# Selective scans in a decoder: one state per step on 128 channels, or four states of 32 channels

## The chip, the cores and the metric

The kernel runs on one NeuronCore of a Trainium2 chip. The core has five engines that run side by side, each from its own queue in order: TensorE (PE in the profile, with its weight loads PEld as a row of their own), VectorE (DVE), ScalarE (ACT), GpSimd (POOL) and SyncE (SP), which issues the DMA transfers. The metric is the device time of one execution in microseconds. Before the change it is 2396.54 us, the median of three runs (2393.58 to 2400.45).

## The reference

Ten layers of a decoder on `x` of 4 sequences x 256 tokens x 256 channels, each ending in a layer norm of the sum. The change touches two of them, `L0_xattn` and `L1_xattn`, both selective state-space layers over the context. Cut to what matters:

```python
u = silu(conv4(in_proj_w @ ctx) + conv_b)               # 256 channels, 256 times, per sequence
dt_lo, Bm, Cm = split(x_proj_w @ u, (8, 16, 16))        # 16 states
delta = softplus(dt_proj_w @ dt_lo + dt_proj_b)
A = -exp(A_log)                                         # 256 channels x 16 states
for t in range(256):
    state = state * exp(delta[t] * A) + (delta[t] * u[t]) * Bm[t]
    y[t] = sum over the 16 states of state * Cm[t]
out = (y + D * u) * silu(x)
```

So for each of 4 sequences, 256 channels and 16 states there is a recurrence over 256 times, and the 16 states of a channel are summed at the end. The layers between them are a multi-query attention (before the first one), a small recurrent block called "thought" and a grouped attention (before the second one), and a mixture of experts after it.

## The kernel before

`Scans` (line 406) holds what the two state-space layers share. `load` brings the weights of a layer, `taps` (431) multiplies the four taps of the convolution with the input projection, so that `conv4(in_proj_w @ ctx)` becomes four matrix products. `_steps` (460) is a Python generator which emits a layer's instructions piece by piece, so that other code can put them beside its own. First it makes `u`, `delta` and `du` = `delta * u`, all with 128 channels on the partitions, two chunks of channels (`DC` = 2) and all 1024 times (4 sequences x 256) along the columns; B and C go to DRAM (`bc`).

Then comes one step for each sequence and state, 64 in a layer. A step loads the B and the C row of its state from DRAM, spread over all 128 partitions (tile `t` named `bc`, 256 KB, four buffers); ScalarE makes `exp(delta * A)` of both chunks (`dA`, three buffers); VectorE multiplies `du` by B into `s`, runs the scan over 512 columns (two chunks of 256 times; a zero in the first column of `dA` starts each chunk afresh), and multiplies by C. Two steps later (`late`) PE adds `s` into a PSUM bank by a product with the identity (`add`, 510). The bank sums the 16 states. After the last state VectorE adds `D * u` and leaves the result in `u`. There is one PSUM bank for all of this (`bank`, 441).

Who calls it: the first layer is begun inside the multi-query attention (`run_mqa`, 367) and goes on with `K.scans.beside(2)` (387) in each of its 32 iterations, two steps an iteration. The second is begun in `run_thought` (727), gets 24 steps at the end of that function (802), and one step at a time in the grouped attention (`run_gqa`, 1059 and 1063). `gate_pair` (549) multiplies a sequence's result by `silu(x)` and adds it to the stream; it first draws on the generator until that sequence is done (`upto`).

The order in which instructions are emitted is a priority and not yet the order on the engines: the framework plans each engine's queue at build time, with its own model of durations, and may move an instruction of a lower priority into a gap that it expects. On the chip each engine then runs its queue strictly in order. This holds for SP as well: a transfer whose memory or data is not ready yet holds up all that are issued after it. Helpers: `K.act` is a ScalarE activation (line 131), `K.tt`, `K.stt`, `K.ts` VectorE operations (116, 125, 120), `K.ptt` GpSimd (128), `K.mm` a matrix product (137). An fp32 matrix product shows as two MATMUL instructions and two weight loads. `again(ap, n)` reads the same columns n times.

Of the kernel before, what the change touches and what calls it, by code (L numbers as in the profile page):

```python
# [19 lines left out]
F32 = mybir.dt.float32  # L20
# [382 lines left out]
SSM_COLS = 19  # L403


class Scans:
    def __init__(self, K, ctx):
# [3 lines left out]
        self.wk = ctx.enter_context(tc.tile_pool(name="ssm2", bufs=4))  # L411
# [3 lines left out]
        self.dA = [self.one.tile([P, DC, L], F32, name=f"dA{k}") for k in range(3)]  # L415
# [6 lines left out]
    def load(self, pre):  # L422
        K = self.K
        self.w[pre] = {
            "in": K.load(self.one, f"{pre}_in", [P, D]),
            "xp": K.load(self.one, f"{pre}_xp", [P, DC, 40], "(c p) n -> p c n", p=P),
            "dt": K.load(self.one, f"{pre}_dt", [8, D]),
            "cols": K.load(self.one, f"{pre}_cols", [P, DC, SSM_COLS], "(c p) n -> p c n", p=P),
        }

    def taps(self, pre):
        K = self.K
        w = self.w[pre]
        w["taps"] = []
        for j in range(4):
            t = self.wk.tile([P, D], F32, name="tap", tag="bc", padded_shape=[P, 2 * L])
            K.nc.sync.dma_start(out=t, in_=K.A[f"{pre}_cw"][:, j * D : (j + 1) * D].to_broadcast([P, D]))
            K.ptt(t, t, w["in"], MUL)
            w["taps"].append(t)
# [20 lines left out]
    def _steps(self, pre):  # L460
        K, nc, w, wk = self.K, self.K.nc, self.w[pre], self.wk
# [3 lines left out]
        delta = self.one.tile([P, DC, N], F32, name="delta")  # L465
        du = self.one.tile([P, DC, N], F32, name="du")
# [5 lines left out]
        for h in range(2):  # L472
            for c in range(DC):
                ps = self.bank()
                for j in range(4):
                    K.mm(ps, taps[j][:, c * P : (c + 1) * P], K.ctxp[:, 2 * h : 2 * h + 2, j : j + L], j == 0, j == 3)
                K.act(u[:, c, 512 * h : 512 * h + 512], ps, AF.Identity, bias=cols[:, c, 0:1])
        K.act(u, u, AF.Silu)
        negA = self.one.tile([P, DC, 16], F32, name="negA")
        K.act(negA, cols[:, :, 2:18], AF.Exp)  # L480
        K.ts(negA, negA, -1.0, None, MUL)
        bc = self.dram.tile([2, 16, N], F32, name="bcd")
        for h in range(2):
            s = slice(512 * h, 512 * h + 512)
            xd = wk.tile([P, 512], F32, name="xd", tag="s")
# [6 lines left out]
            for c in range(DC):  # L492
# [3 lines left out]
                K.ts(delta[:, c, s], ps, cols[:, c, 1:2], None, ADD)  # L496
                K.act(du[:, c, s], ps, AF.Abs, bias=cols[:, c, 1:2])
        K.act(du, du, AF.Exp, scale=-1.0)
        K.act(du, du, AF.Ln, bias=K.eps[1.0])
        for c in range(DC):  # L500
            K.stt(delta[:, c, :], delta[:, c, :], 0.0, du[:, c, :], MAX, ADD)
            K.tt(du[:, c, :], delta[:, c, :], u[:, c, :], MUL)

        turn = 0
        self.y = u

        late = []
        bank = {}

        def add(b, n, s):  # L510
            if n == 0:
                bank[b] = self.bank()
            y = bank[b]
            K.mm(y, K.ident, s.rearrange("p c l -> p (c l)"), n == 0, n == 15)
            if n == 15:
                for c in range(DC):
                    v = u[:, c, b * L : (b + 1) * L]
                    K.stt(v, v, cols[:, c, 18:19], y[:, c * L : (c + 1) * L], MUL, ADD)
                self.done += 1

        for b in range(B):
            lo = b * L
            for n in range(16):
                yield
                if len(late) > 1:
                    add(*late.pop(0))
                t = wk.tile([P, 2, L], F32, name="bc", tag="bc")
                nc.sync.dma_start(out=t, in_=bc[:, n, lo : lo + L].unsqueeze(0).to_broadcast([P, 2, L]))
                dA = self.dA[turn % 3]
                turn += 1  # L530
                for c in range(DC):
                    K.act(dA[:, c, 1:L], delta[:, c, lo + 1 : lo + L], AF.Exp, scale=negA[:, c, n : n + 1])
                s = wk.tile([P, DC, L], F32, name="s")
                K.tt(s, du[:, :, lo : lo + L], again(t[:, 0, :], DC), MUL)
                nc.vector.tensor_tensor_scan(  # L535
                    out=s.rearrange("p c l -> p (c l)"),
                    data0=dA.rearrange("p c l -> p (c l)"),
# [1933 lines left out]
```

## Time and profile before

| what | value |
|---|---|
| median of three runs | 2396.54 us |
| the profiled execution | 2403.96 us, span 2402.2 us |
| granted TensorE clock, mean | 0.947 |
| 0 to 64 us | loads, first products of attention, `u`, `delta`, `du` of the first layer |
| 64 to 347 us | scans of the first layer, beside the multi-query attention |
| 347 to 409 us | end of attention, `u`, `delta`, `du` of the second layer, start of "thought" |
| 409 to 441 us | scans of the second layer beside "thought" |
| 441 to 468 us | end of "thought" |
| 468 to 701 us | scans of the second layer, beside the grouped attention from about 495 |

How to read it. "Busy" is the time in which an engine runs an instruction; a group row gives the line, the engine, the operation, the tiles written and read, the shapes (partitions x columns), the count, the busy time in us and the mean duration in ns, then the idle time of the engine before these instructions and what ended it. A row of the timeline begins with start and duration in us. A row of the waits says who waited for whom, the sum in us, how often, and the longest. In a row on stretches of time, "(x...)" is the number of instructions, and the numbers after the engines are the granted clock of TensorE, the DMA share and GB/s.

### The profile page before, as it was taken

The page shows a single profiled execution, that of the slowest core. Times are in us where ns is not written, and L with a number is a line of the kernel's source. Part 1 is how long each engine was busy: PE and PEld are TensorE (multiplying, and loading weights), DVE is VectorE, ACT ScalarE, POOL GpSimd, SP SyncE. Part 2 cuts the span into 40 slices and gives each one's busy share as a digit, 9 for nine tenths or more (in the row PEclk, how much of TensorE's full clock was granted, in tenths as well). Part 3 has the DMA queues.
Part 4 walks back from the last instruction along what each step waited for, and adds up shares of the span by engine and source line. Part 5 has one row for each costly group of instructions (what it writes and reads, how often), then busy time and mean ns, then how long its engine had stood idle before and what let it go on. Part 6 is the DMA issues. An engine that isn't in the chain of part 4 may idle for free. (4 is left out here: it accounts for less than half of the span.)

```text
span 2402.2 us, 28595 instructions
## 1 busy us (share of the span) xinstructions
PE 2227.1 (93%) x10504; PEld 1516.5 (63%) x10504; DVE 1461.9 (61%) x3178; ACT 787.2 (33%) x1763; POOL 260.4 (11%) x419
## 2 busy tenths in 40 slices
PE   8899998589987999899999999999999988899998
PEld 4566763335434655536888888888776545477676
DVE  4999975999876121380465544445565658686466
ACT  5677765223432011261211111111122223253443
POOL 1000010220010322200101000110110001200001
PEclk9999998788987999999999999999998888999999
DMA  7222221222213644220222111111100021100000
GB/s 224 62 55 60 48 66 31 56 70 53 49 36 94 195 129 125 77 72 5 75 86 87 47 47 56 66 47 49 48 22 1 1 77 43 42 1 1 1 1 18
DMA packets 133747, 139.50 MB, mean 58 GB/s; under 512 B 13892, under 2 KB 121766, under 8 KB 131944
## 3 DMA queue, kind: packets, MB, share of 16 engines
q1 hardware_dynamic: 133608, 137.68, 20.0%
q8 instruction: 83, 1.36, 0.2%
q14 instruction: 56, 0.46, 0.1%
HBM read 134.79 MB, written 2.85 MB: 57 GB/s over the span
## 5 line engine op out<-in xcount | busy, mean ns | idle before, releaser
L137 PE MATMUL ps<-xw,xcT 128*128 128x256 f32 (+1 forms) x2304 | 518.9, 382 | 0.3 <-ACT YT L131 0.3
L137 PEld LDWEIGHTS ps<-xw,xcT 128*128 128x128 f32 x2304 | 430.8, 190 | 64.0 <-issue 1.9
L116 DVE TENSOR_TENSOR xp<-ps,xb 128x256 f32<-128x256 f32 x96 | 40.5, 422 | 232.1 <-PE ps L137 232.0
L137 PE MATMUL sc<-kT,qT 32*128 32x256 f32 (+2 forms) x768 | 167.5, 412 | 10.0 <-DVE qn L134 9.7
L131 ACT ACTIVATE dA<-delta,negA 128x255 f32<-128x255 f32 x256 | 118.5, 501 | 131.1 <-DVE s L535 129.4
L137 PE MATMUL ssmps<-s,idz 128*128 128x512 f32 x256 | 143.7, 670 | 17.1 <-DVE s L116 16.0
L535 DVE TENSOR_TENSOR_SCAN s<-dA,s 128x512 f32<-128x512 f32 x128 | 154.6, 1219 | 2.6
L137 PEld LDWEIGHTS sc<-kT,qT 32*128 32x128 f32 (+1 forms) x768 | 106.9, 204 | 73.4 <-issue 45.2
L116 DVE TENSOR_TENSOR hT<-u,a 128x512 f32<-128x512 f32 x48 | 33.2, 691 | 186.0 <-PE u L137 184.9
L131 ACT ACTIVATE sq<-xp 128x1024 f32<-128x1024 f32 x24 | 25.4, 1057 | 314.1 <-DVE xp L116 314.1
L174 POOL TENSOR_SCALAR rstd<-mv 128x2 f32<-128x2 f32 x48 | 11.6, 241 | 951.9 <-DVE mv L166 932.7
L134 DVE TENSOR_REDUCE qn<-sc 128x2 f32<-128x480 f32 (+1 forms) x192 | 87.2, 506 | 39.1 <-PE sc L137 38.1
L131 ACT ACTIVATE e<-sT 128x512 f32<-128x512 f32 x128 | 70.9, 590 | 112.0 <-PE sT L137 109.9
L137 PE MATMUL sT<-q,kT 32*128 32x256 f32 (+1 forms) x384 | 103.4, 518 | 3.4 <-ACT e L131 3.3
L1503 DVE TENSOR_TENSOR_SCAN dec<-xT,idz 128x256 f32<-128x256 f32 (+1 forms) x192 | 89.8, 537 | 19.0 <-DMA xT<-ad 19.0
L131 ACT ACTIVATE a<-g 128x512 f32<-128x512 f32 x48 | 28.7, 599 | 206.4 <-PE g L137 206.4
L137 PE MATMUL g<-xT,wj 128*128 128x512 f32 x192 | 92.1, 603 | 0.7 <-ACT rows L105 0.7
L137 PE MATMUL u<-xT,wj 128*128 128x512 f32 x192 | 90.9, 595 | 0.0
L137 PEld LDWEIGHTS y<-wj,hT 128*128 128x128 f32 x384 | 73.0, 190 | 26.6 <-issue 18.2
L116 DVE TENSOR_TENSOR s<-du,bc 128x512 f32<-128x512 f32 x128 | 87.7, 694 | 2.7 <-PE ssmps L137 2.5
L137 PE MATMUL ps<-xT,wi 128*128 128x512 f32 x192 | 85.7, 603 | 4.0 <-ACT xin L131 4.0
L137 PE MATMUL y<-wj,hT 128*128 128x256 f32 x384 | 89.2, 379 | 0.0
(504 smaller groups left out, 4057.4 us busy)
## 6 DMA issues: line engine op xcount, KB each, us to landing
bc<-bcd SPq DMA_DIRECT2D x128, 256.0 KB, 4.5
xw<-in_l2a_xw_dram SPq DMA_DIRECT2D x24, 768.0 KB, 4.9
xT<-ad SPq DMA_DIRECT2D x12, 1024.0 KB, 4.5
wj<-in_l1f_gate_dram SPq DMA_DIRECT2D x48, 128.0 KB, 2.9
wj<-in_l1f_up_dram SPq DMA_DIRECT2D x48, 128.0 KB, 2.8
wj<-in_l1f_down_dram SPq DMA_DIRECT2D x48, 128.0 KB, 3.0
sel<-cwd SPq DMA_DIRECT2D x32, 192.0 KB, 3.3
sel<-cwd SPq DMA_DIRECT2D x32, 128.0 KB, 3.2
```

What stands on the lines that cost most here:

```text
L116: self.nc.vector.tensor_tensor(out=out, in0=a, in1=b, op=op)
L131: self.nc.scalar.activation(out, in_, func, **kw)
L134: self.nc.vector.tensor_reduce(out=out, in_=in_, axis=AX.X, op=op, **kw)
L137: self.nc.tensor.matmul(out, lhsT=lhsT, rhs=rhs, start=start, stop=stop)
L174: self.nc.gpsimd.tensor_scalar(out=out, in0=in_, scalar1=add, scalar2=None, op0=ADD)
L535: nc.vector.tensor_tensor_scan(out=s.rearrange("p c l -> p (c l)"), data0=dA.rearrange("p c l -> p (c l)"), data1=s.rearrange("p c l -> p ...
L1503: nc.vector.tensor_tensor_scan(out=dec[:, k, h, :], data0=ap[:, h, at(bb, k, j) : at(bb, k, 2)], data1=K.idz[:, 0 : (2 - j) * P], initial=0.0,
```

## The change

A step now holds 32 channels x 4 states on the 128 partitions (partition 4 x channel + state) and four groups of 32 channels along the columns, each with its 256 times: 1024 columns. A step is one sequence, one chunk of 128 channels and one set of four states: 4 x 2 x 4 = 32 steps in a layer. The number of scanned values is the same.

For that `delta` and `du` must be spread over four partitions per channel. They are put side by side in the tile `pair` (one per chunk), stored to DRAM (`dd`, 1 MB a chunk), and loaded back for each sequence and chunk with every channel's row repeated four times: eight loads of 128 KB into the new `t` (two buffers, shared with `pair` and `taps`), which serves the four steps of its chunk. B and C of four states are loaded once per sequence (`bct`, one buffer for each set, two loads of 128 KB), spread over 32 channels, and serve both chunks. `dA` has two buffers of 1024 columns, `s` four. The generator now yields twice in a step: before the loads, exponentials and product with B, and again before `add`, the scan and the product with C; so a call of `beside(1)` emits half a step, and there are still 64 calls in a layer.

The sum over the states is now also a sum over four partitions. `pick` is a matrix of zeros with a 32-column band in the middle that takes partition 4 c + state to column c. In the first layer each group's product has only the 32 columns of the band and writes 32 partitions of the bank; in the second layer each group takes 128 columns of `pick`, shifted so that the band lies at the group's 32 partitions and the rest adds zeros. Both are four products of 256 columns a step. The Exp and Ln of softplus run for each chunk apart.

```diff
-SSM_COLS = 19
+SSM_COLS = 3
+SN = 4
...
-        self.wk = ctx.enter_context(tc.tile_pool(name="ssm2", bufs=4))
+        self.wk = ctx.enter_context(tc.tile_pool(name="ssm2", bufs=2))
+        self.sp = ctx.enter_context(tc.tile_pool(name="ssm3", bufs=4))
...
-        self.dA = [self.one.tile([P, DC, L], F32, name=f"dA{k}") for k in range(3)]
+        self.dA = [self.one.tile([P, 4, L], F32, name=f"dA{k}") for k in range(2)]
...
+            "alog": K.load(self.one, f"{pre}_alog", [P, DC * 16]),
         }
+        if not hasattr(self, "pick"):
+            self.pick = K.load(self.one, "ssm_pick", [P, 2 * P - 32])
...
-        w["taps"] = []
+        w["taps"] = self.wk.tile([P, 4, D], F32, name="taps", tag="dd", padded_shape=[P, 8, D])
         for j in range(4):
-            t = self.wk.tile([P, D], F32, name="tap", tag="bc", padded_shape=[P, 2 * L])
+            t = w["taps"][:, j, :]
...
         bc = self.dram.tile([2, 16, N], F32, name="bcd")
+        dd = self.dram.tile([D, 2, N], F32, name="ddd")
+        pair = [self.wk.tile([P, 2, N], F32, name="pair", tag="dd") for _ in range(DC)]
...
-                K.ts(delta[:, c, s], ps, cols[:, c, 1:2], None, ADD)
-                K.act(du[:, c, s], ps, AF.Abs, bias=cols[:, c, 1:2])
-        K.act(du, du, AF.Exp, scale=-1.0)
-        K.act(du, du, AF.Ln, bias=K.eps[1.0])
+                K.ts(pair[c][:, 0, s], ps, cols[:, c, 1:2], None, ADD)
+                K.act(pair[c][:, 1, s], ps, AF.Abs, bias=cols[:, c, 1:2])
         for c in range(DC):
-            K.stt(delta[:, c, :], delta[:, c, :], 0.0, du[:, c, :], MAX, ADD)
-            K.tt(du[:, c, :], delta[:, c, :], u[:, c, :], MUL)
+            K.act(pair[c][:, 1, :], pair[c][:, 1, :], AF.Exp, scale=-1.0)
+        for c in range(DC):
+            K.act(pair[c][:, 1, :], pair[c][:, 1, :], AF.Ln, bias=K.eps[1.0])
+        for c in range(DC):
+            delta, du = pair[c][:, 0, :], pair[c][:, 1, :]
+            K.stt(delta, delta, 0.0, du, MAX, ADD)
+            K.tt(du, delta, u[:, c, :], MUL)
+            nc.sync.dma_start(out=dd[c * P : (c + 1) * P], in_=pair[c])
...
-        def add(b, n, s):
-            if n == 0:
+        def add(b, c, m, s):
+            if (c, m) == (0, 0):
                 bank[b] = self.bank()
             y = bank[b]
-            K.mm(y, K.ident, s.rearrange("p c l -> p (c l)"), n == 0, n == 15)
-            if n == 15:
+            for g in range(4):
+                at = slice(c * L, (c + 1) * L)
+                if pre == "l0x":
+                    K.mm(y[32 * g : 32 * g + 32, at], self.pick[:, P - 32 : P], s[:, g, :], c + m == 0, c + m == 4)
+                else:
+                    lo = P - 32 - 32 * g
+                    K.mm(y[:, at], self.pick[:, lo : lo + P], s[:, g, :], c + m + g == 0, (c, m, g) == (1, 3, 3))
+            if (c, m) == (DC - 1, 3):
...
         for b in range(B):
-            lo = b * L
-            for n in range(16):
-                yield
-                if len(late) > 1:
-                    add(*late.pop(0))
-                t = wk.tile([P, 2, L], F32, name="bc", tag="bc")
-                nc.sync.dma_start(out=t, in_=bc[:, n, lo : lo + L].unsqueeze(0).to_broadcast([P, 2, L]))
-                dA = self.dA[turn % 3]
-                turn += 1
-                for c in range(DC):
-                    K.act(dA[:, c, 1:L], delta[:, c, lo + 1 : lo + L], AF.Exp, scale=negA[:, c, n : n + 1])
-                s = wk.tile([P, DC, L], F32, name="s")
-                K.tt(s, du[:, :, lo : lo + L], again(t[:, 0, :], DC), MUL)
-                nc.vector.tensor_tensor_scan(
...
-                K.tt(s, s, again(t[:, 1, :], DC), MUL)
-                late.append((b, n, s))
+            at = slice(b * L, (b + 1) * L)
+            for c in range(DC):
+                for m in range(4):
+                    yield
+                    if m == 0:
+                        t = self.wk.tile([P, 2, 4, L], F32, name="dd", tag="dd")
+                        for j in range(2):
+                            for g in range(4):
+                                rows = dd[c * P + 32 * g : c * P + 32 * g + 32, j, at]
+                                nc.sync.dma_start(out=t[:, j, g, :], in_=rows.unsqueeze(1).to_broadcast([32, SN, L]))
+                    if c == 0:
+                        bct = self.one.tile([P, 2, L], F32, name=f"bct{m}")
+                        for k in range(2):
+                            rows = bc[k, SN * m : SN * m + SN, at]
+                            nc.sync.dma_start(out=bct[:, k, :], in_=rows.unsqueeze(0).to_broadcast([32, SN, L]))
+                        sets = [bct] if m == 0 else sets + [bct]
+                    dA = self.dA[turn % 2]
+                    turn += 1
+                    for g in range(4):
+                        q = 16 * c + 4 * g + m
+                        K.act(dA[:, g, 1:L], t[:, 0, g, 1:L], AF.Exp, scale=negA[:, q : q + 1])
+                    s = self.sp.tile([P, 4, L], F32, name="s")
+                    K.tt(s, t[:, 1], again(sets[m][:, 0, :], 4), MUL)
+                    yield
+                    if len(late) > 1:
+                        add(*late.pop(0))
+                    flat = s.rearrange("p g t -> p (g t)")
+                    nc.vector.tensor_tensor_scan(
...
+                    K.tt(s, s, again(sets[m][:, 1, :], 4), MUL)
+                    late.append((b, c, m, s))
```

## The prediction

> **What bounds the kernel now.** I read the page first, then busy time by stretches, the same for the scan tile `s` alone, the groups with shapes kept apart, the timeline of a dense stretch, and last the DMA issues and SP's waits. The page's shares and VectorE's busy tenths (one digit per 60 us):
> ```profile
> PE 2227.1 (93%) x10504; PEld 1516.5 (63%) x10504; DVE 1461.9 (61%) x3178; ACT 787.2 (33%) x1763; POOL 260.4 (11%) x419
> DVE  4999975999876121380465544445565658686466
> ```
> The 93% of PE is an average over the whole program. The change touches the first 720 us only, and there VectorE's digits are the nines. By stretches (us; PE, weight loads, DVE, ACT, POOL busy; clock; DMA), first for everything, then for tile `s` (PE, weight loads, DVE):
> ```profile
> 64.00:346.00 282.00, 264.64 (x1168) 184.61 (x1169) 267.80 (x445) 200.38 (x574) 11.51 (x18) 0.99 0.25 58
> 409.00:441.00 32.00, 24.44 (x119) 10.88 (x120) 28.85 (x45) 19.69 (x40) 2.77 (x2) 0.79 0.38 85
> 441.00:468.00 27.00, 7.44 (x30) 5.01 (x28) 24.42 (x74) 2.40 (x5) 14.09 (x22) 0.66 0.06 9
> 500.00:700.00 200.00, 187.64 (x1027) 89.99 (x1026) 178.66 (x288) 79.72 (x162) 21.16 (x42) 0.86 0.23 49
> ```
> ```profile
> 64.00:346.00 282.00, 60.57 (x128) 23.44 (x128) 156.80 (x192) 0.99 0.25 58
> 409.00:441.00 32.00, 14.41 (x22) 4.25 (x22) 28.02 (x36) 0.79 0.38 85
> 441.00:468.00 27.00, 0.00 (x0) 0.00 (x0) 1.60 (x2) 0.66 0.06 9
> 500.00:700.00 200.00, 47.84 (x74) 12.67 (x74) 102.00 (x118) 0.86 0.23 49
> ```
> The first layer's scans lie in 64 to 346 beside the first attention, the second layer's in 409 to 701. VectorE is busy 267.8 of 282 us in the first, and more than half of that is scans. PE is nearly as full, but VectorE has only 14.2 us of gaps. From 409 to 441 VectorE does almost nothing but scans; from 441 to 468 it has none.
>
> What one step costs. Groups (count, busy us, mean ns), then a dense stretch of the timeline (start, us), where steps follow each other with no wait:
> ```profile
> L535 DVE TENSOR_TENSOR_SCAN s<-dA,s 128x512 f32<-128x512 f32 x128 | 154.6, 1219 | 2.6
> L1503 DVE TENSOR_TENSOR_SCAN dec<-xT,idz 128x256 f32<-128x256 f32 x96 | 60.3, 674 | 19.0 <-DMA xT<-ad 19.0
> L116 DVE TENSOR_TENSOR s<-du,bc 128x512 f32<-128x512 f32 x128 | 87.7, 694 | 2.7 <-PE ssmps L137 2.5
> L116 DVE TENSOR_TENSOR prod<-rows,hot 128x1024 f32<-128x1024 f32 x4 | 4.9, 1220 | 2.9 <-ACT rows L105 2.8
> ```
> ```profile
> 414.61 0.67 DVE L116 TENSOR_TENSOR s<-du,bc 128x512 f32<-128x512 f32 x1
> 415.19 0.69 DVE L116 TENSOR_TENSOR s<-s,bc 128x512 f32<-128x512 f32 x1
> 415.79 1.22 DVE L535 TENSOR_TENSOR_SCAN s<-dA,s 128x512 f32<-128x512 f32 x1
> 416.93 0.67 DVE L116 TENSOR_TENSOR s<-du,bc 128x512 f32<-128x512 f32 x1
> ```
> From start to start a step takes 416.93 - 414.61 = 2.32 us, though its three durations add to 2.58: each instruction overlaps the next by 0.087 us. So VectorE pays little per instruction, and much per column.
>
> **The change, part by part.**
>
> (1) VectorE: two steps of 512 columns become one of 1024. A 1024-column product is 1.22 us (row `prod`). No scan of 1024 is in the trace; from 256 to 512 columns a scan grows by 545 ns, so 512 more add 1.09: 2.31 us. The big step is 1.22 + 1.22 + 2.31 = 4.75, less three overlaps of 0.087 = 4.49, against 2 x 2.32 = 4.64. That saves 0.15 x 32 steps = 4.8 us a layer, 9.6 in both. By durations without overlap (694 + 1219 + the 686 of the other product = 2.60 a step) it would be 5.20 - 4.75 = 0.45, 14.3 a layer: the upper bound. The lower bound is a loss: where a scan follows its own product, as at 338.98 to 339.70, nothing overlaps, and big steps of 4.75 in such a row would cost 0.11 more than two small ones overlapped, 3.5 a layer. I take 4.8, since the stretches that count run dense.
> [...]
>
> (2) The start of each layer. Before, the first product (64.1 in the first layer) follows 0.5 us after `du` is complete. Now `delta` and `du` go through DRAM. The Ln is split by chunk; a 1024-column ACT instruction takes 1.06 (row `sq`) where the 2048-column one took 2.00, so chunk 0 of the pair is ready at about 60.4 in place of 63.6. Then: the issue 0.4, the 1 MB store, then eight loads of `t` and two of `bct` on SP, 0.45 each = 4.5, and the last lands 2.9 later. SP also issues the second 1 MB store ahead of these loads. For the store I have transfers of 1 MB:
> ```profile
> xT<-ad SPq DMA_DIRECT2D x12, 1024.0 KB, 4.5
> wj<-in_l1f_gate_dram SPq DMA_DIRECT2D x48, 128.0 KB, 2.9
> w_d<-in_l0f_d_dram SPq DMA_DIRECT2D x1, 1024.0 KB, 8.1
> ```
> First product at 60.8 + 4.5 + 7.4 = 72.7, or 76.3 with 8.1: 8.6 to 12.2 us late; I take 10.4 (the second store is between). At worst the 14.9 us of the loaded `x` transfer: 19. In the first layer attention's VectorE work fills some of it: scans are 156.8 of 282 there, so 56% is lost, +5.8 (bounds 0, if attention runs ahead, and 19). In the second, scans are 28.0 of 32 us and nothing replaces them: +9.1 (0 to 19).
>
> (3) SP's order. In the second layer SP stood still, and the scan loads behind it:
> ```profile
> SPq L148 <- DVE gate L125: 25.2, 1, 25.2
> ```
> This is the router's load waiting for memory; the hole at 441 to 468 is its trace. One `t` now covers four big steps and there are two; `bct` covers two chunks. Steps can go on through the hole, and VectorE's idle there is 27 - 24.4 = 2.6: -2.6 (0 to -2.6). In the steady run, a layer issues 64 + 32 loads where it issued 64, 96 x 0.45 = 43 us of SP time in some 280: no bound. Single-buffered `bct` m is freed three steps before its next use (13 us or more, against 3 to 4.5 to land), `t` four steps before: no wait. The two loads more ahead of the taps push these back by 0.9: +0.5 (0 to 0.9).
>
> (4) PE. First layer: the four 512-column instructions of two steps take 1.88 us; eight band instructions, by this row of another stage,
> ```profile
> 590.22 1.05 PE L137 MATMUL o<-e,vt 128*32 128x256 f32 x16
> ```
> about 0.6, since four bands run at once. PE gets 32 x 1.28 = 41 us free, off the path: VectorE's waits for PE between 64 and 346 add to 1.5 us. -1.5 (0 to -14.2, all of VectorE's gaps). Second layer: eight of 256 columns at full width take 1.89 as in attention's rows, as much as four of 512: 0.
> PE's granted clock is 0.99 where PE is 94% busy and 0.66 where it is 28% busy. The bands take 41 us of its 264.6 away. At the clock of 500 to 700 the rest would need 224 x 0.99/0.86 = 258 us, still under VectorE's; at 0.79 it would need 281 and be level.
> [...]
>
> (5) Larger blocks in VectorE's queue. A reduction behind a scan waits up to 2.31 in place of 1.22. Between 500 and 700 lie 118/6 = 20 big steps: 0 to 20 x 1.09 = 22 us, and no gain, since no bank comes free earlier. VectorE works meanwhile; loss comes only when PE, freed late, leaves it dry. PE's weight loads waited 9.7 us for `qn` there, 14 times: I take +2. ACT's exponentials are as many and as long; two `dA` of a big step hold more than three small ones: 0.
>
> Sum: -9.6 + 5.8 + 9.1 - 2.6 + 0.5 - 1.5 + 2 = +3.7. The profiled execution took 2403.96 (span 2402.2 and 1.8 around it), 7.4 above the median of 2396.5: 2407.7 by it, 2400 by the median. 0.3% (7 us) is about what a measurement tells from no change.
>
> **The rivals.**
> Faster: the round trips are hidden. For: attention's work can run ahead of scans that are late, and the second layer has 2.6 + 21 us of idle later. Against: at 409 nothing else is ready. Without terms (2), -9.6 - 2.6 - 1.5 + 2 = -12: 2385; with the 14.3 of the durations in both layers, 2366.
> Slower: the blocks decide. One mechanism: in the second attention the score reductions stand behind 2.3 us scans, PE cannot refill its three score banks, VectorE runs dry when the scan is over. For: PE is busy 187.6 and VectorE 178.7 of 200, so neither has room, and the clock is already 0.86. Against: scans can be moved between reductions. 20 blocks at 1.09 less the 2 counted: +20, 2420. It decides from 11 us, half of that, on.
> The change moves nothing: VectorE's sum falls only by instruction overheads, and the starts give this back: 2390 to 2404, inside my forecast.
>
> **How the numbers follow.** Forecast, a draw with a small loss, 2389 to 2410: 0.47, of which 0.25 within 0.3% and 0.22 slower. Faster rival, 2366 to 2389: 0.33. Slower rival, 2410 to 2425 and above: 0.20. So faster 0.33, same 0.25, slower 0.42. The range leaves out a tenth on each side: 2378 to 2424; the likeliest case alone has 2389 to 2410.
>
> **What would show it.** Scans of 1024 columns at 2.3 us and products at 1.22; first product of a layer 8 to 12 us after `du`; between 64 and 346 PE's busy time some 40 us lower at a clock still near 0.99, the stretch about 280 long; scans going on while the router's load waits; PE's waits for `qn` near 10 us. I am wrong if VectorE stands idle behind `t` loads in the middle of a layer, if the clock in the first layer falls under 0.8, or if scans take other than 2.1 ns a column.

## The result, and the profile after

The changed kernel takes 2417.98 us in the median of 18 runs (2402.98 to 2436.44), the kernel before 2403.39 us beside it (18 runs, 2393.36 to 2413.92). The ratio is 1.0067, with a 95% interval of 1.0039 to 1.0095: slower by some 16 us. The profiled execution took 2433.68 us (span 2431.9). Executions of one kernel spread over 16 to 36 us here, and in the profiles up to 20 us of this lie behind the two layers, in code that no kernel here changes: from the first weight load of a later stage (`xw`) to the end it is 1292 to 1295 us in most, 1312 in three, this one among them, and 1301 in that of before. So I compare lengths of stages up to that mark as well as medians.

Three stages hold the change: A, up to SP's load of the grouped attention's weights (end of the first attention); B, from there to the load of the router's weights (thought); C, from there to the load of `sim` (the grouped attention). Their ends before are 353.27, 464.76 and 713.10 us, after 348.72, 456.25 and 731.85. Busy time by stage (us; PE, weight loads, VectorE, ScalarE, GpSimd; clock, DMA share, GB/s), A counted from 64 us. Before:

```profile
64.00:353.27 289.27, 271.91 (x1199) 189.77 (x1200) 268.67 (x447) 202.04 (x577) 12.78 (x19) 0.99 0.25 57
353.27:464.76 111.49, 77.01 (x360) 38.66 (x359) 72.89 (x162) 47.24 (x75) 22.37 (x35) 0.84 0.20 46
464.76:713.10 248.34, 224.96 (x1160) 105.45 (x1161) 216.14 (x353) 93.35 (x191) 27.19 (x52) 0.85 0.24 53
```

After:

```profile
64.00:348.72 284.72, 258.45 (x1346) 172.86 (x1345) 265.06 (x355) 202.55 (x594) 22.46 (x19) 0.97 0.18 47
348.72:456.25 107.53, 74.67 (x348) 39.94 (x346) 55.69 (x132) 43.55 (x66) 22.09 (x35) 0.79 0.20 60
456.25:731.85 275.60, 244.16 (x1302) 146.82 (x1303) 224.67 (x287) 97.70 (x203) 26.71 (x52) 0.80 0.13 35
```

A is 4.6 us shorter, B 4.0 shorter, C 27.3 longer: +18.7. Now take VectorE's busy time from each length. Its work shrank by 557.7 - 545.4 = 12.3 us. Its idle time went from 20.6 to 19.7 in A, from 38.6 to 51.8 in B, and from 32.2 to 50.9 in C: +31.0. So VectorE has less to do, as the larger instructions should give, and more idle time came in, none of it in the first layer's stage A. In stage C the last product of the layer ends at 701.00 us before, at 706.61 after: of the 27.3 us, 14.1 lie ahead of that product and 13.1 behind it, where VectorE has little left to do.

The lines that answer those of the prediction are these. The stretches for everything, then for tile `s` (PE, weight loads, VectorE):

```profile
64.00:346.00 282.00, 255.85 (x1329) 170.89 (x1327) 264.12 (x353) 202.55 (x594) 22.46 (x19) 0.97 0.18 47
409.00:441.00 32.00, 22.14 (x122) 13.05 (x122) 19.06 (x36) 16.34 (x32) 7.00 (x10) 0.71 0.32 99
441.00:468.00 27.00, 10.69 (x35) 7.33 (x36) 23.51 (x60) 1.23 (x3) 10.06 (x16) 0.56 0.05 10
500.00:700.00 200.00, 187.19 (x1049) 110.67 (x1049) 171.23 (x228) 76.41 (x162) 20.77 (x42) 0.81 0.12 32
```

```profile
64.00:346.00 282.00, 24.04 (x248) 5.86 (x248) 152.00 (x96) 0.97 0.18 47
409.00:441.00 32.00, 2.16 (x8) 1.44 (x8) 11.46 (x7) 0.71 0.32 99
441.00:468.00 27.00, 5.67 (x16) 3.83 (x16) 6.98 (x6) 0.56 0.05 10
500.00:700.00 200.00, 43.86 (x141) 30.82 (x141) 95.50 (x62) 0.81 0.12 32
```

Between 409 and 441 VectorE has 11.5 us of scan work where it had 28.0. Three big steps, as wide as six small ones, are scanned before the router's load, where 13 small ones were.

The groups (count, busy us, mean ns), and a dense stretch of VectorE's timeline (start, us):

```profile
L560 DVE TENSOR_TENSOR_SCAN s<-dA,s 128x1024 f32<-128x1024 f32 x64 | 146.3, 2292 | 6.0 <-ACT dA L131 5.0
L116 DVE TENSOR_TENSOR s<-dd,bct 128x1024 f32<-128x1024 f32 x64 | 77.9, 1226 | 12.5 <-PE ssmps L137 12.0
```

```profile
463.35 2.35 DVE L116 TENSOR_TENSOR s<-dd,bct 128x1024 f32<-128x1024 f32 x2
465.62 4.47 DVE L560 TENSOR_TENSOR_SCAN s<-dA,s 128x1024 f32<-128x1024 f32 x2
470.00 2.34 DVE L116 TENSOR_TENSOR s<-s,bct 128x1024 f32<-128x1024 f32 x2
472.25 2.35 DVE L116 TENSOR_TENSOR s<-dd,bct 128x1024 f32<-128x1024 f32 x2
```

Two big steps take 472.25 - 463.35 = 8.90 us, 4.45 each. The second row of the groups shows a wait of VectorE's: the first product of a step needs a free `s`, and PE's sum is what frees it.

SP's queue and VectorE's at the start of the second layer, and last VectorE's first product there before:

```profile
403.68 5.43 SPq L510 DMA_DIRECT2D ddd<-pair  x2
409.20 11.26 SPq L542 DMA_DIRECT2D dd<-ddd  x16
```

```profile
419.67 3.50 DVE L116 TENSOR_TENSOR s<-dd,bct 128x1024 f32<-128x1024 f32 x3
424.96 2.29 DVE L560 TENSOR_TENSOR_SCAN s<-dA,s 128x1024 f32<-128x1024 f32 x1 [1.80 <-ACT dA L131]
```

```profile
409.41 0.69 DVE L116 TENSOR_TENSOR s<-du,bc 128x512 f32<-128x512 f32 x1
```

Both stores and the second chunk's eight loads are in front, and a load of `dd` takes SP 11.26 / 16 = 0.70 us. The first product starts at 419.67, where it started at 409.41.

VectorE's waits for PE's sums in stage C (who for whom, us, times, longest), before:

```profile
DVE u L125 <- PE ssmps L137: 8.0, 2, 6.9
DVE s L116 <- PE ssmps L137: 2.3, 3, 1.6
```

and after:

```profile
DVE u L125 <- PE ssmps L137: 14.1, 3, 11.8
DVE s L116 <- PE ssmps L137: 12.0, 8, 2.6
```

One is the wait for a finished bank, the other that for a free buffer `s`. Together they are 26.1 us against 10.3.

### The profile page after: what moved, and what is told of

Its sections match the earlier page's. It is cut to its first block, busy times and chain, and to the rows that moved or that the text cites. A ratio compares the mean times of both kernels' runs of the same rounds, so it can differ in the third digit from the quotient of the medians.

```text
span 2431.9 us, 28936 instructions
## 1 busy us (share of the span) xinstructions
PE 2241.8 (92%) x10760; PEld 1546.1 (64%) x10760; DVE 1447.4 (60%) x2986; ACT 786.3 (32%) x1770; POOL 269.5 (11%) x418
## 5 line engine op out<-in xcount | busy, mean ns | idle before, releaser
L137 PE MATMUL sc<-kT,qT 32*128 32x256 f32 (+2 forms) x768 | 182.0, 437 | 14.9 <-DVE qn L134 9.8
L137 PEld LDWEIGHTS sc<-kT,qT 32*128 32x128 f32 (+1 forms) x768 | 113.1, 215 | 77.9 <-issue 44.8
L560 DVE TENSOR_TENSOR_SCAN s<-dA,s 128x1024 f32<-128x1024 f32 x64 | 146.3, 2292 | 6.0 <-ACT dA L131 5.0
L131 ACT ACTIVATE dA<-dd,negA 128x255 f32<-128x255 f32 x256 | 112.6, 500 | 97.6 <-DVE s L560 97.5
L137 PE MATMUL ssmps<-s,w_ssm_pick 128*32 128x256 f32 (+1 forms) x512 | 103.8, 431 | 22.2 <-DVE s L116 21.1
L174 POOL TENSOR_SCALAR rstd<-mv 128x2 f32<-128x2 f32 x48 | 12.1, 252 | 955.3 <-DVE mv L166 925.1
L137 PEld LDWEIGHTS ssmps<-s,w_ssm_pick 128*32 128x32 f32 (+1 forms) x512 | 62.7, 171 | 56.7 <-DVE s L116 29.3
```

Of the source, the lines that this page charges most:

```text
L131: self.nc.scalar.activation(out, in_, func, **kw)
L137: self.nc.tensor.matmul(out, lhsT=lhsT, rhs=rhs, start=start, stop=stop)
L174: self.nc.gpsimd.tensor_scalar(out=out, in0=in_, scalar1=add, scalar2=None, op0=ADD)
L560: nc.vector.tensor_tensor_scan(out=flat, data0=dA.rearrange("p g l -> p (g l)"), data1=flat, initial=0.0, op0=MUL, op1=ADD,)
```

## Experiments

First all of them. Each median stands beside that of the kernel before in the same session (2398.65 for the first four, 2403.67 for the next four, 2404.20 for e9 to e11, 2404.42 for e12). The last column is where the first weights `xw` are loaded into PE in the profile.

| kernel | median us | ratio to before, 95% | A | B | C | xw at |
|---|---|---|---|---|---|---|
| before | | | 353.3 | 111.5 | 248.3 | 1100.8 |
| the change | 2417.98 | 1.0067 [1.0039, 1.0095] | 348.7 | 107.5 | 275.6 | 1119.6 |
| e1 first layer only | 2398.97 | 1.0016 [0.9989, 1.0043] | 346.4 | 104.6 | 260.4 | 1099.8 |
| e2 second layer only | 2415.14 | 1.0076 [1.0047, 1.0105] | 354.7 | 107.0 | 267.2 | 1116.6 |
| e3 bands in both | 2411.72 | 1.0046 [1.0019, 1.0073] | 346.8 | 107.0 | 270.4 | 1107.9 |
| e4 full width in both | 2425.88 | 1.0122 [1.0086, 1.0158] | 368.1 | 106.7 | 266.7 | 1129.4 |
| e5 half blocks | 2411.82 | 1.0024 [1.0003, 1.0045] | 355.7 | 105.1 | 272.4 | 1116.7 |
| e6 early begin, 8 steps | 2418.64 | 1.0036 [1.0003, 1.0069] | 346.7 | 132.0 | 240.3 | 1106.7 |
| e7 the same with bands | 2405.58 | 1.0004 [0.9976, 1.0031] | 349.9 | 132.0 | 240.3 | 1110.3 |
| e8 before, early begin, 16 steps | 2399.90 | 0.9992 [0.9967, 1.0017] | 352.9 | 121.3 | 242.6 | 1104.3 |
| e9 as e1, 13 steps ahead of the gates | 2417.40 | 1.0039 [1.0012, 1.0067] | 347.4 | 120.2 | 251.4 | 1102.3 |
| e10 sums one step earlier | 2401.57 | 0.9999 [0.9971, 1.0027] | 347.6 | 106.9 | 259.6 | 1101.1 |
| e11 as e6, no round trip | 2406.01 | 1.0011 [0.9977, 1.0044] | 348.4 | 118.9 | 246.6 | 1101.7 |
| e12 e10 with early begin | 2415.70 | 1.0041 [1.0014, 1.0068] | 348.1 | 112.1 | 257.8 | 1105.3 |

Stages are of one execution each. Where the same stage should be alike it differs by up to 3.5 us (A from 346.4 to 349.9 where the first layer is that of the change), so I read nothing smaller. C differs by more: e2 and e4 have the second layer of the change, with as many of its scans in C (29), and take 267 us there in place of 275.6.

My theories were these. T1: the late start of the second layer pushes scans out of thought, where VectorE idles, into the attention, where it does not. T2: the sums of the second layer hold up PE and, through the `s` buffers, VectorE. T3, my slower rival: scans of 2.3 us (the blocks) keep reductions waiting. T4: only the granted clock differs.

**Which layer (e1, e2).** The new steps in one layer and the old in the other.

```diff
-        self.left = self._steps(pre)
+        self.left = (self._steps if SSM_COLS[pre] == 3 else self._steps_old)(pre)
```

> First layer with the new steps (32 channels x 4 states, bands), second layer with the steps of before (128 channels, one state, sum by the identity). The profile of the change puts the whole loss behind the router's load (456 to 732 us, 27 us longer than before) and a gain of 4.6 us ahead of it. If the loss is made by the second layer's steps, whatever their mechanism, this kernel takes 2403 - 5 = 2398 us (2393 to 2403), and the stretch from the router's load to the next layer's first load is 248 us again. If it is the granted clock alone that differs between the two profiles, this kernel lies within 3 us of the changed one, 2415 to 2421.

> First layer with the steps of before, second layer with the new ones (full-width sums). If the second layer's steps make the loss: 2403 + 16 + 5 = 2424 us (2418 to 2430), and the stretch from the router's load to the next layer's first load is about 275 us. If the two layers only gain and lose by the overlap of their starts and ends with attention (the first late by 14.5 us, the second by 10.3), each alone gives half of the change's 15 us: 2410.

The first layer alone moves the whole by nothing that can be measured, the second alone costs 16.5 us in the medians, as much as the change (14.6). T4 falls: e1 lies at 2399, not at 2415 to 2421. The first layer's steps keep their gain in A, 6.9 us here. But e1's C is 260.4 us with the old steps, 12.1 longer than before, and its B 6.9 shorter. The numbers of scans say why: 7 small steps stand ahead of the router's load, 57 behind it, where the kernel before has 13 and 51. The build-time planner places other steps there when the first layer changes. So some 12 us in C can come without any new step in the second layer, 7 of which B gives back.

**Width of the sums (e3, e4).**

```diff
-                if pre == "l0x":
+                if pre:        # e3; e4: if not pre:
```

> The changed kernel with the sums of the second layer in bands as well (32 columns of weights, 32 partitions of the bank, as in the first layer). The sums of the second layer fall from 77 us of PE to about 32 x 0.64 = 20 to 30. If full-width sums are what holds the second attention up (PE busy 244 of 276 us, scan tiles held by PE 12 us, exponentials waiting 74 us for PE's scores), 20 us and more come back: 2395 to 2402. If the late start of 10.3 us and the displaced scans make it, PE's time there is not the limit: 2413 to 2420. If the clock is set by how much of the array PE uses, bands lower it (0.80 in this stretch, then under 0.77) and the time is 2418 to 2430.

> The changed kernel with full-width sums in the first layer as well. By my step (4) bands free some 41 us of PE in the first layer, off the path. Then full width puts them back: PE busy 256 + 32 x (1.99 - 0.64) = 299 us in a stretch of 282, so PE becomes the bound there and the first layer is 10 to 17 us longer: 2428 to 2435. If the sums fit into PE's waits for scans and the clock gains by the fuller array, the first layer stays within 3 us: 2415 to 2421.

Full width in the first layer makes A 19.4 us longer, a little more than the 10 to 17 expected; the median is 27.2 us above that of the kernel before in its session, 12.6 more than the change's, since C is shorter here than in the change. The sums' PE time there goes from 24.87 to 61.88 us, the same as the 62.04 of the identity products before, but A is 14.9 us longer than before. One thing that differs from before is the number of weight loads: 48.69 us of them for the sums in place of 24.20. That these make the 14.9 us is not shown; the late start is in them too.

Bands in the second layer take the sums from 77.0 to 28.6 us of PE, and C gets only 5.2 us shorter. Stage C of e3:

```profile
453.79:724.18 270.39, 222.01 (x1307) 107.33 (x1307) 223.21 (x287) 97.39 (x203) 23.57 (x52) 0.70 0.12 36
```

PE has 48 us less of sums but only 22 us less of work: the rest of its work went from 167 to 193 us, and its granted clock from 0.80 to 0.70. VectorE's waits for sums nearly vanish: those for the bank are not among the eight longest, those for `s` are 3.5 us. Others come in their place (`rec` and `qn` belong to the attention):

```profile
DVE rec L969 <- PE o L137: 13.2, 3, 10.0
DVE qn L134 <- PE sc L137: 11.1, 6, 3.6
```

T2 in the form "PE has too much to do" falls, and the waits for sums cannot simply be subtracted from C either. The median, 2411.7, is 13.1 us above that of the kernel before in its session, the change's 14.6; it is nearest to the second expectation. That the clock falls with bands was the third; that the kernel gets slower by it did not come true.

**Block size (e5).** Two products and scans of 512 columns in place of one of 1024, all else as in the change.

```diff
-                    K.tt(s, t[:, 1], again(sets[m][:, 0, :], 4), MUL)
+                    for g in (0, 2):
+                        K.tt(s[:, g : g + 2, :], t[:, 1, g : g + 2], again(sets[m][:, 0, :], 2), MUL)
...
+                    for g in (0, 2):
+                        half = s[:, g : g + 2, :]
```

> The changed kernel with the layout, the loads and the sums of the change, but each of a step's products and scans as two instructions of 512 columns, so that a reduction waits behind 1.2 us and not 2.3. If the blocks decide (my slower rival), the attention beside the second layer's scans gets back 20 us and the smaller instructions cost the 9.6 us of my step (1): 2408. If the loss is in the displaced scans or in the sums, only the 9.6 us are lost: 2418 + 10 = 2428 (2424 to 2432).

A gets 7.0 us longer, B and C together 5.7 shorter (383.1 to 377.4). VectorE's busy time in A rises from 265.06 to 273.84 us with 96 instructions more: 91 ns per instruction. The median, 2411.8, is 6 us under the change's and lies between the two expectations, 2408 and 2428, nearer to T3's. But e2 and e4, which have large blocks in the second layer, need 374.2 and 373.4 us in B and C, less than e5. So a gain from smaller blocks is not shown and not excluded. The place that I named for it shows no loss that they could give back: PE's weight loads waited 9.7 us for `qn` between 500 and 700 us before, and in the change 8.6:

```profile
PEld sc L137 <- DVE qn L134: 8.6, 11, 1.5
```

**Displaced steps (e6, e7, e8, e9).** The second layer is begun ahead of thought's chain, and steps are emitted between the gates of thought, so that eight big ones (16 small ones in e8) stand ahead of the router's load.

```diff
+        K.scans.begin("l1x")
         last = K.tp.tile([B, D], F32, name="last", tag="tp")
...
-        K.scans.begin("l1x")
...
                 ahead = gated(b + 1)
+            K.scans.beside(4)
             added(b, *this)
-        K.scans.beside(24)
+        K.scans.beside(8)
```

> The changed kernel with the second layer begun ahead of thought's chain and with eight of its big steps in VectorE's queue before the end of that chain, where the change has three. What is computed in each step is the same. If the loss is scans displaced into the attention by the late start (in the changed kernel 29 of 32 big steps stand there, in the kernel before 51 of 64 small ones, which is 3.5 big steps fewer), five steps x 4.46 = 22 us leave the attention stage, 276 to some 254, and thought gets longer by at most half of it, since VectorE idles for 51 of its 107 us: 2402 to 2411. If full-width sums on PE hold up the attention, it stays above 265 and thought is longer: 2418 to 2425.

> The same early begin and eight steps, with the sums of the second layer in bands. If displaced scans and sums are two separate costs, this takes the 6 us of the bands and the 7 to 16 us of the early begin together: 2396 to 2404. If both relieve the same wait, it gives no more than the better of them alone.

> The kernel before with the second layer begun as early and 16 small steps (the columns of eight big ones) before the end of thought, where it had 13. If displacement is the price, three small steps x 2.32 = 7 us leave the attention stage and thought is longer by up to half: 2396 to 2400. If the old kernel's thought is already held up by its scans, it is 2400 to 2406.

C does what T1 says: 275.6 to 240.3. But B grows by 24.4, not by "at most half" of 22. `xw` begins 12.9 us earlier, and yet the median is that of the change, 2418.6, while e7, whose `xw` begins 3.6 us later than e6's, has a median 13 lower: the twelve runs of e6 lie between 2393 and 2427, and its median says little. e7 missed its 2404 by little, and e8 is where both its cases meet. In the old kernel three more small steps ahead of the router's load make B 9.8 longer and C 5.8 shorter. T1 is right about where the steps are, and wrong about their price: steps put into VectorE's idle time in thought lengthened thought by about as much as they weigh, since thought's own short operations then stood behind the scans. e6 and e8 also give a fair comparison of the second layer's steps, since the same columns stand in the same stage: C is 240.3 with the new steps and 242.6 with the old, and B is 132.0 against 121.3. So with equal placement the new steps are no slower beside the attention, although VectorE's waits for sums are 23.7 us there against 10.3, and cost 10.7 us in thought; both stages together 8.4. e7 shows no gain from bands once fewer steps stand in C (240.3 both), with a clock of 0.74 against 0.86.

In e9 the first layer is new, the second old, and 13 small steps are emitted ahead of the first gate.

```diff
+        K.scans.beside(13)
         ahead = gated(0)
...
-        K.scans.beside(24)
+        K.scans.beside(11)
```

> As the kernel with only the first layer new, but 13 of the second layer's old small steps are emitted ahead of thought's gates, the number that the kernel before has there (in the kernel with only the first layer new 7 stood there, and the attention stage took 260.4 us against 248.3). If the gain of the first layer (346.4 against 353.3 us) was lost through six displaced steps, the two stages from the second layer's weights to the next layer's first load take 360 us again in place of 365, and the whole 2403 - 7 = 2396 us, 0.3% under the kernel before (2391 to 2400). If the displaced steps are not what the attention stage depends on, it stays at 2399 to 2403.

This missed: B and C take 371.6 us, not 360. VectorE's timeline of e9:

```profile
426.69 0.14 DVE L885 COPY lastmean<-last 128x4 f32<-128x4 f32 x1
...
427.42 0.16 DVE L116 TENSOR_TENSOR thT<-ps,lastmean 128x8 f32<-128x8 f32 x1
...
443.73 1.22 DVE L648 TENSOR_TENSOR_SCAN s<-dA,s 128x512 f32<-128x512 f32 x1
444.87 0.39 DVE L116 TENSOR_TENSOR gate<-gate,ps 128x256 f32<-128x256 f32 x1
```

`thT` is what the products for thought's gates are made from. It begins at 427.42, and the first gate comes 17.5 us later, with scans and products of the steps between them in VectorE's queue. In the kernel before `thT` came at 438.99, and the first gate 3.5 us later, at 442.51. From the first gate to the router's load both kernels take 22 to 23 us. Here scans were cheap only until the chain reached its gates; against e1, six steps more make B 15.6 us longer and C 9.0 shorter. The median of 2417.4 is worse than either expectation, which the stages do not show: `xw` begins only 2.5 us later than in e1, whose median is 2399.0.

**The round trip (e11).** As e6, but without the second layer's stores. Its loads take the first layer's `delta` and `du` instead, so it computes other values with equal shapes.

```diff
...
+            if pre == "l0x":
                 nc.sync.dma_start(out=dd[c * P : (c + 1) * P], in_=pair[c])
```

> As the kernel with the early begin and eight steps ahead of thought's end, but the second layer leaves out its two stores of delta and du and loads the first layer's delta and du instead, which lie in DRAM already. Its second layer computes from wrong delta and du, everything else and every shape is the same. The first product came 9.7 us after the first pair in the early kernel (403.9 to 413.6); without the stores the loads can be issued when the first pair is done, at 398.4: first product at about 407.5. If the trip is what thought's stage pays for (132.0 us there, 121.3 in the old kernel with the same columns placed as early), 4 to 8 us of the 10.7 go: 2407 to 2414 against 2418.6. If the stage is held up by something else, it stays at 130 us and more.

The first product comes at 408.97 in place of 413.62, the expectation was 407.5. B is 13.0 us shorter and C 6.3 longer, with seven steps ahead in place of eight: 6.7 us in both together, inside the expected 4 to 8. The median is 2406.0 against 2418.6. So the round trip costs some 7 of the 8.4 us by which e6 exceeds e8 in both stages, read from one profile each.

**Late sums (e10, e12).** The sum of a step is emitted two steps after its scan, as before, and a step is now twice as wide. In e10 it comes one step after, in the second layer.

```diff
-                    if len(late) > 1:
+                    if len(late) > (pre == "l0x"):
```

> The changed kernel with the sums of a step of the second layer emitted one step after its scan and not two, so that its buffer comes free earlier and fewer sums are left for the end. VectorE's waits for PE's sums in the attention stage were 12.0 us for buffers of s and 14.1 us for the finished bank, against 2.3 and 8.0 before. If late sums are a cost of their own, some 10 us of these 16 go: 2406 to 2412. If PE is simply full there, the waits only change their place: 2414 to 2422.

> The changed kernel with the second layer's sums emitted one step after their scan, and the second layer begun ahead of thought's chain, with no step forced in between thought's gates (four big steps then stand ahead of the gates, three in the changed kernel). In the kernel with early sums alone the second layer's stages took 106.9 and 259.6 us, with three steps ahead of the gates. If the steps ahead of the gates use idle time and those between the gates cost more than they weigh (eight forced ahead of thought's end made thought 24.5 us longer for five steps), the attention stage loses one more big step, 259.6 - 4.5 = 255, and thought stays at 107 to 110: 1 to 4 us under the kernel with early sums, about 2399, level with the kernel before or 0.2% under it (2394 to 2403). If thought's chain is held up by the second layer's products on PE when these stand ahead of it, thought takes 112 and more and nothing is won: 2401 to 2406.

C falls from 275.6 to 259.6 us, more than the 10 us expected, and the ratio to 0.9999, with an interval clear of the change's. (That of e7, 1.0004, is too, with the sums late; the ratio alone does not single them out.) VectorE's idle time in C goes from 50.9 to 35.3 us, near the 32.2 of before, at the same work:

```profile
454.47:714.05 259.58, 228.65 (x1302) 139.29 (x1303) 224.30 (x287) 97.57 (x203) 24.63 (x52) 0.86 0.13 37
```

```profile
DVE s L116 <- PE ssmps L137: 8.0, 7, 2.6
DVE u L125 <- PE ssmps L137: 7.2, 3, 5.2
```

The two waits add to 15.2 in place of 26.1 us, 10.9 less. The layer's last product ends 11.7 us earlier in the stage, and 4.3 us are gained behind it. Of the 10.9, some 4.5 belong to the first part and 6.5, the wait for the last bank (11.8 to 5.2), to the second. So the waits for sums are 4.5 of the 11.7; the rest there is less work of VectorE's (2.3) and other waits. Behind the last product PE's timeline shows what else happens. PE in the change:

```profile
706.14 1.99 PE L137 MATMUL ssmps<-s,w_ssm_pick 128*128 128x256 f32 x8
711.97 0.69 PE L584 MATMUL ps<-idz,gate 128*128 128x128 f32 x2 [3.83 <-POOL gate L128]
...
714.72 2.07 PE L137 MATMUL sT<-q,kT 32*128 32x512 f32 x2
...
719.77 1.94 PE L137 MATMUL o<-e,ones 128*32 128x256 f32 x16
...
724.97 4.58 PE L137 MATMUL ssmps<-s,w_ssm_pick 128*128 128x256 f32 x20
```

and in e10 (the first line is VectorE's last product):

```profile
691.87 1.22 DVE L116 TENSOR_TENSOR s<-s,bct 128x1024 f32<-128x1024 f32 x1
...
701.48 0.44 PE L584 MATMUL ps<-idz,gate 128*128 128x128 f32 x2 [0.51 <-POOL gate L128]
702.04 1.12 PE L137 MATMUL sT<-q,kT 32*128 32x512 f32 x2
...
705.10 1.07 PE L137 MATMUL o<-e,ones 128*32 128x256 f32 x16
```

The transposes of the third sequence's gate (L584) wait for GpSimd, GpSimd for ScalarE, and ScalarE for the layer norm of `x`, whose operations on VectorE stand among the steps:

```profile
702.55 0.42 DVE L116 TENSOR_TENSOR x<-ps,x 128x256 f32<-128x256 f32 x1
702.88 2.28 DVE L560 TENSOR_TENSOR_SCAN s<-dA,s 128x1024 f32<-128x1024 f32 x1
705.08 0.40 DVE L165 BATCH_NORM_STATS2 stats<-x 128x6 f32<-128x256 f32 x1
705.40 1.21 DVE L116 TENSOR_TENSOR s<-s,bct 128x1024 f32<-128x1024 f32 x1
706.52 0.18 DVE L166 BATCH_NORM_AGGREGATE mv<-stats 128x2 f32<-128x6 f32 x1
```

The statistics come 2.1 us late behind a scan and their aggregate 1.0 late behind a product. PE stops for 3.83 us at the transposes. After that two `sT` products take 2.07 us in place of 1.12, sixteen `o` products 1.94 in place of 1.07. In e10 the last scan begins at 689.5, ahead of that norm, and PE stops for 0.51. The granted clock of the change from 712 to 724 us:

```profile
712.00:724.00 12.00, 12.00 (x50) 5.52 (x52) 2.80 (x8) 2.75 (x5) 0.93 (x2) 0.50 0.01 2
```

In e10 it is 1.00 from 702 to 714. In the change the clock is 0.50 from 711 us on, less than 3 us after PE's last product ended at 708.13 and ahead of the next. In the kernel before it fell after a gap of 2.27 us (last section).

The stop is not that of one profile: it is 3.7 to 3.8 us in all kernels with the new steps in the second layer, late sums and whole blocks (e2, e3, e4, e6, e7, e11), 3.1 with half blocks (e5), 0.5 in e10 and e12, and 2.3 with the old steps (before, e1, e8, e9). From the layer's last product to the end of C it is 21 to 25 us in the first group, 20.1 in e5, 21.0 in e10 and e12, and 9 to 14 with the old steps.

How much of the 16 us is typical stays open. e2 and e4, with sums as late, have 267 us in C; by them the early sums are worth 7. e12, which has the early sums too, has a C of 257.8 us with one scan fewer in it (28); with 4.45 us for that one they would be worth 5, an estimate. Its B is 112.1 and its `xw` begins 4.2 us later than in e10: nothing is won by the early begin, as its second expectation said; whether PE's products are the reason is not shown. Its median of 2415.7 was not expected and is not explained by the stages, so the medians of e10 and e12 show less than the stages, and the ratio of e10 may flatter it. More buffers `s`, the other way to take these waits away, were not tried.

No kernel here beats the one before by more than can be measured; e10 is level with it, and so are e1, e7, e8 and e11.

## Why the prediction was right or wrong

The range, 2378 to 2424, held 2418 by its width: the sum gave a loss of 3.7 us, and the change cost some 16. The likeliest case, 2389 to 2410, did not hold it. The time lies where the slower rival was priced, but what it named, reductions that leave PE without score banks, was not seen: the place found where a block made PE stop is the norm at 703 us. Seven us of it are the base: the kernel before measured 2403.4 beside the change, and 2396.5 in the three runs that I started from.

(1) VectorE's larger instructions: right, a little small. A scan of 1024 takes 2.29 us (forecast 2.31), a product 1.22 to 1.24 (1.22), a step 4.45 in a dense run (4.49). VectorE's work fell by 12.3 us in the three stages (forecast 9.6). The half blocks cost 91 ns per instruction in the first layer, more than the 50 ns that my sum has for one (0.15 us a big step for three instructions fewer).

(2) The late start: the delay was right in the second layer (10.3 us, forecast 10.4) and too small in the first (14.5 us, inside the bound of 19); SP spent 0.70 us on a load of `dd`, where I took 0.45. The match in the second layer is luck: A ended 4.6 us earlier, and counted from its end the first product comes 14.8 us later than before, as in the first layer. The price was wrong in the first layer: VectorE's idle time there did not grow at all, attention's work ran ahead, and A became 4.6 us shorter where my terms for it add to zero. In the second layer VectorE's idle time in B grew by 13.2 us, against 9.1; yet B became 4.0 us shorter.

(3) SP's order: wrong. Steps did not go on through the hole: the third scan ended at 434.05 us and the fourth began at 465.6, although SP had issued the `dd` loads of eight steps by 420.5. In VectorE's queue the gates of thought stood ahead of the scans. The hole was not SP's, and -2.6 us did not come.

(4) PE: in the first layer the sums fell from 62.0 to 24.9 us as forecast, at a clock of 0.97: one band product lasts 0.38 us or more, but 257 of them take 24.87 us together, 0.097 each, so they do overlap; at full width (e4) it is 61.88 us for 259, 0.239 each. But PE's whole time from 64 to 346 us fell by 8.8 us only, not by 40: the rest of its work took longer, as in e3. And their worth was misjudged: I called this time off the path, and with full width (e4) A is 19 us longer. In the second layer "as much as four of 512: 0" held for the products: PE's time for sums in C went from 68.4 to 77.0 us, but for the columns of 62 small steps in place of 53, which is 1.24 us a small step in place of 1.29. It left out the weight loads, which went from 19.0 to 55.3 us; that these cost time was not shown, since C lost only 5 us when they fell to 6.6 (e3).

(5) Coarser blocks: this is the step that failed most, in its second half. The reductions wait as I said (8.6 us for `qn`, I wrote "near 10"). But I costed the buffers at nothing, with `dA` as the only one in view, and the end of the layer not at all. `s` and the bank are held until PE's sum, the sum was still emitted two steps later, and a step is now 4.45 us and not 2.32. VectorE's waits for sums in C grew by 15.8 us; with the sums one step earlier 10.9 of them went, and C lost 16 us (e10). And the end of the layer became 13.1 us longer, with a stop of PE behind a block, and half clock, in it. That the late sums are the cause of the loss is not fully shown: the waits also went with bands, and C lost 5 us only (e3); they were nearly as long in e6 (23.7 us), whose C is no longer than the old steps' in e8; and e2, with 28.3 us of them, has a C 8 us under the change's. What is shown is that the loss comes with the second layer's new steps (e1, e2), and that the order in which the same work stands in the queues decides over some 5 to 16 us of it.

What my sum lacked altogether is the planner: a change of the first layer alone moved six small steps of the second from thought into the attention (e1), 12 us in C against 7 in B, and e2 and e4 differ from the change by 8 to 9 us in C with the same second layer.

## What to carry to other kernels

When a step is made twice as large, everything that is counted in steps becomes twice as long: lags, the time that a buffer is held, prefetch. Recount them in microseconds before the step's own cost. And before filling an engine's idle time with other work, look whether that engine's short operations, on which a chain hangs, would then queue behind it: here five steps, 22 us, lengthened the chain by 24.

## What the runs showed of the hardware

Sums in bands of 32 columns lowered the clock that PE was granted in the attention, from 0.80 to 0.70 (e3) and from 0.86 to 0.74 (e7), with PE busy for 82 and 86% of the stage. Whether the narrower products do this, or the gaps that PE has when it has less to do, is not shown. In the first layer it was 0.97 with bands and 0.97 without (e4), with PE busy for 91 and 92% of the stage.

A gap of 2.27 us on PE, at 697 us of the kernel before, was followed by half clock: from 699 to 705 us it is 0.50, and two `sT` products take 2.07 us in place of 1.12. In e1 a gap of 2.28 us was not: two `sT` products behind it take 1.12 us. So the length of a gap alone does not decide here. Before, then e1:

```profile
697.08 0.44 PE L559 MATMUL ps<-idz,gate 128*128 128x128 f32 x2 [2.27 <-POOL gate L128]
...
700.55 2.07 PE L137 MATMUL sT<-q,kT 32*128 32x512 f32 x2
```

```profile
698.40 0.44 PE L673 MATMUL ps<-idz,gate 128*128 128x128 f32 x2 [2.28 <-POOL gate L128]
...
701.05 1.12 PE L137 MATMUL sT<-q,kT 32*128 32x512 f32 x2
```

A load of 128 KB that repeats each channel's row four times took SP 0.70 us where sixteen followed each other and 0.63 where eight did (464.63 us, 5.05 us), in place of the 0.45 that I had taken for any load.
